# Turning the x tiles of a projection: TensorE transpositions, or VectorE's 32x32 blocks put together by transfers

## The chip, the cores and the metric

One core of a Trainium2 chip runs the whole program in one launch. The metric is the device time of a run in microseconds (us). The kernel before takes 3609.12 us in the median of three runs.

## What is computed

A transformer layer on x of shape [8, 1024, 512], float32. First attention with a low-rank latent (MLA): the layer-normed x is projected to a query latent and a key/value latent of 128 columns each and to a rotary key of 16. Sixteen heads are built from the latents, with causal softmax. Then a feed-forward part whose weights and activations are quantized to FP4 in blocks of 16 and dequantized again. Cut to what matters here:

```python
x = x + attn(layernorm(x), W_DQ, W_UQ, W_QR, W_DKV, W_UK, W_UV, W_KR, W_O)
x = x + ffn(layernorm(x), w_gate, w_up, w_down)

# in attn
c_q  = x @ W_DQ          # [B, S, 512] @ [512, 128]
c_kv = x @ W_DKV         # [B, S, 512] @ [512, 128]
Kr   = rope(x @ W_KR)    # [B, S, 512] @ [512, 16]
...
return attn @ W_O
# in ffn
h = silu(fp4_linear(x, w_gate)) * fp4_linear(x, w_up)
return fp4_linear(h, w_down)
```

The three products with x contract over its 512 columns, and TensorE contracts over partitions. So each normed tile of 128 rows x 512 columns must be turned: its columns have to come to lie along the partitions. The change is about this turning.

## The kernel before, in words

**Units.** The 8 x 1024 rows are cut into 16 units of 512 rows (`U`), two to a sequence: even units are the first half, odd ones the second. A unit is four tiles of 128 rows. While the attention of unit u runs (`attention`), the projections of unit u+1 are made (`project_pieces`), and so is a share of the feed-forward work of earlier units (`ffn_pieces`). An even unit has 4 quads of heads x 3 score steps, an odd one 4 x 7, and odd units take 13 parts of the feed-forward work where even ones take 5. In units 0 to 3 the raw feed-forward weights are quantized and turned in place of feed-forward work (`weight_pieces`: three loads and 34 pieces, which go through `turn`, line 186).

**The order.** The order on TensorE, VectorE and ScalarE is written out by hand. A piece is a pair of a cost and a function. `merged` interleaves a unit's own pieces with its share of other work, so that both lists advance by the same share of their cost. `attention` runs a score step and then pieces for as long as the cost of the pieces run, with half of the next one, stays below the share of the unit that its score steps have reached. A piece's cost so decides where it lands, and a cost that has no TensorE work behind it takes the place of some that has. A small model of time, `Clock`, decides where VectorE's deferred work (quantizing, adding up softmax sums) is laid in between. The order on SyncE's queue (SP), which issues nearly all DMAs, and on GpSimd is not written out: the framework chooses it, and places a DMA where its inputs and its buffer are ready.

**The projection of a unit** (`project_pieces`), for each of two pairs of tiles: `fetch` loads two x tiles (line 160, buffer tag xl, two buffers). `norms(0)` takes the statistics on VectorE (lines 320 to 322) and the power on GpSimd (323); `norms(1)` scales in place (326). `rows_turned` turns a tile with four TensorE transpositions into a PSUM bank and one ScalarE copy into xnT (`turn`, lines 186 and 188). `rotation` multiplies xnT by the rotary key weights (tile pr) and by the key/value latent weights (pp, wdkv); `rotated` does the query latent (pp, wdq) and the fold of the rotary key (pf). All TensorE products other than transpositions go through `mm` and have line 114.

**wo.** In the third score step of a unit's first quad, `fetch_wo` (lines 707 to 709) claims one of three softmax buffers (tag pT), which has to be given back by the product that reads it (num) and by the addition that sums it (line 599), and loads the 1 MB output weights into it. At the end of the same step `out_proj` multiplies by them (tile po), after `fillers` of that step:

```python
score_step(u, hq, j, qc, qr, acc, aT)
flush(1)
if urgent and j == 2:
    fetch_wo()
...
while fillers and (gone + fillers[0][0] / 2) * whole < total * spent:
...
while urgent and j == 2:
    urgent.popleft()()
```

`out_proj` loads x again (tag xo, 160), adds it on VectorE (728), and stores the sum to a DRAM tile mid (730), from which the feed-forward part reads it (y, line 747; xr, 823). `down` ends with the store of the result (852).

Of the kernel before, what the change touches and what calls it, by code (L numbers as in the profile page):

```python
# [11 lines left out]
F32 = mybir.dt.float32  # L12
# [6 lines left out]
P = 128  # L19
B, S, D = 8, 1024, 512  # L20
# [5 lines left out]
U = 512  # L26
NT = U // P
NDC = D // P
# [14 lines left out]
def tile_mla_then_fp4_ffn(  # L43
# [17 lines left out]
    nc = tc.nc  # L61
    const = ctx.enter_context(tc.tile_pool(name="const", bufs=1))
    p1 = ctx.enter_context(tc.tile_pool(name="p1", bufs=1))
    p2 = ctx.enter_context(tc.tile_pool(name="p2", bufs=2))
# [15 lines left out]
    class Clock:  # L80
# [3 lines left out]
        shape = None  # L84
# [23 lines left out]
    clk = Clock()  # L108

    def mm(dst, par=1, **kw):  # L110
        shape = kw.get("tile_position", ()) and "rows" or dst.shape[0]
        clk.pe += 0.00168 * dst.shape[-1] / par + (0.1 if shape != clk.shape else 0.0)
        clk.shape = shape
        nc.tensor.matmul(dst, **kw)  # L114

# [41 lines left out]
    def load_x(u, t, pool, tag):  # L157
        b, rows = rows_of(u, t)
        xt = pool.tile([P, D], F32, tag=tag, name=f"{tag}_{u}_{t}")
        nc.sync.dma_start(out=xt, in_=x[b, rows, :])  # L160
        return xt


    xls = {(0, t): load_x(0, t, p2, ("xl", "y")[t // 2]) for t in range(NT)}
    by_chunk = lambda w: w.rearrange("(c p) n -> p c n", p=P)
    by_head = lambda w: w.rearrange("p (h n) -> p h n", n=64)
    of_four = lambda w: w.unsqueeze(0).to_broadcast([4, *w.shape])
# [11 lines left out]
    def bank(name):  # L179
        return ps_t.tile([P, 512], F32, tag="t", name=name)  # L180

    def turn(src, dst, n):

        pt = bank("pt").rearrange("p (n k) -> p n k", k=P)
        for i in range(n):
            nc.tensor.transpose(pt[:, i, :], src[:, i * P : (i + 1) * P], ident)
            clk.pe += 0.11
        on_act(0.56, lambda: nc.scalar.copy(dst, pt[:, 0:n, :]))
# [123 lines left out]
    def normed(xt, key):  # L312
        got = {}

        def stats():
            pool, tag = (small, "nx") if key[0] == "x" else (p1, "ny")
            own = pool.tile([P, 10], F32, tag=tag, name=tag)
            st, ve = own[:, 0:6], own[:, 8:9]
            got["mv"], got["rstd"] = mv, rstd = own[:, 6:8], own[:, 9:10]
            nc.vector.bn_stats(st, xt)  # L320
            nc.vector.bn_aggr(mv, st)
            nc.vector.tensor_scalar(ve, mv[:, 1:2], EPS, None, ALU.add)
            nc.gpsimd.tensor_tensor(rstd, ve, neg_half, ALU.pow)

        def scaled():
            nc.vector.tensor_scalar(
                xt, xt, got["mv"][:, 0:1], got["rstd"], ALU.subtract, ALU.mult
            )

        return [(0.9, stats, key), (0.5, scaled, key)]  # L330
# [11 lines left out]
    def project_pieces(u):  # L342
        hf = u % 2
        state = {}

        def fetch(*ts):
            for t in ts:
                if (u, t) not in xls:
                    xls[u, t] = load_x(u, t, p2, "xl")

        def norms(k, *ts):

            for t in ts:
                if k == 0:
                    state["norm", t] = normed(xls[u, t], ("x", u, t))
                cost, run, _ = state["norm", t][k]
                clk.dve += cost
                run()
                state["ready", t] = clk.dve

        def rows_turned(t):
            g, k = divmod(t, 2)
            if k == 0:
                state["xnT"] = p1.tile([P, NDC, 256], F32, tag="xnT", name=f"xnT_{u}_{g}")
            normed_at = state["ready", t]
            clk.pe = max(clk.pe, normed_at)
            turn(xls.pop((u, t)), state["xnT"][:, :, k * P : (k + 1) * P], NDC)

        def latent(g, w, dst):
            cols = slice(g * 256, (g + 1) * 256)  # L370
            pp = bank("pp")
            for i in range(NDC):
                mm(
                    pp[:, :256],
                    lhsT=w[:, i, :],
                    rhs=state["xnT"][:, i, :],
                    start=(i == 0),
                    stop=(i == NDC - 1),
                )
            copy_out(dst[:, cols], pp[:, :256])  # L380

        def rotation(g):
            if g == 0:
                proj[u] = tuple(
                    pool.tile([P, U], F32, tag=tag, name=f"{tag}_{u}")
                    for pool, tag in ((p2, "cq"), (p2, "ckv"), (p3, "kr"))
                )
            pr = bank("pr")
            for i in range(NDC):
                mm(  # L390
                    pr[32 * i : 32 * i + 32, :256],
                    par=4,
                    lhsT=wkr[:, i, :],
                    rhs=state["xnT"][:, i, :],
                    start=True,
                    stop=True,
                )

            krp = proj[u][2][:, g * 256 : (g + 1) * 256]
            tab = rope_sb[:, hf * U + g * 256 : hf * U + (g + 1) * 256]  # L400
            on_dve(
                0.4, clk.pe + 0.3, lambda: nc.vector.tensor_tensor(krp, pr[:, :256], tab, ALU.mult)
            )
            state["krp"] = krp
            latent(g, wdkv, proj[u][1])

        def rotated(g):
            latent(g, wdq, proj[u][0])
            pf = bank("pf")
            for i in range(4):  # L410
                mm(
                    pf[32 * i : 32 * i + 32, :256],
                    par=4,
                    lhsT=fold_sb,
                    rhs=state["krp"],
                    start=True,
                    stop=True,
                )
            copy_out(proj[u][2][:, g * 256 : (g + 1) * 256], pf[:, :256])

        def both(*fs):
            for f in fs:
                f()

        if u == 0:
            for t in (0, 2):
                for k in range(2):
                    norms(k, t, t + 1)
            first, second = [], []
        else:  # L430
            first = [
                (1.0, lambda: fetch(0, 1)),
                (1.5, lambda: norms(0, 0, 1)),
                (3.0, lambda: norms(1, 0, 1)),
            ]
            second = [lambda k=k: norms(k, 2, 3) for k in range(2)]
        return [
            *first,
            (0.5, lambda: rows_turned(0)),
            (0.5, lambda: both(lambda: rows_turned(1), *[lambda: fetch(2, 3)] * (u > 0))),  # L440
            (2.3, lambda: both(lambda: rotation(0), *second[:1])),
            (2.2, lambda: both(lambda: rotated(0), *second[1:])),
            (2.0, lambda: None),
            (0.5, lambda: rows_turned(2)),
            (0.5, lambda: rows_turned(3)),
            (2.3, lambda: rotation(1)),
            (2.2, lambda: rotated(1)),
        ]
# [296 lines left out]
    def fetch(n):  # L745
        ys[n] = p2.tile([P, D], F32, tag="y", name=f"y_{n}")
        nc.sync.dma_start(out=ys[n], in_=mids[tiles[n]])
# [165 lines left out]
    n_weights = len(weight_work)  # L913
# [4 lines left out]
    for u in range(n_units):  # L918
        if u > 0:
            urgent.extend(lambda t=t, aTs=aTs: out_proj(u - 1, t, aTs) for t in range(NT))  # L920
        own = []
        if u + 1 < n_units:
            own.extend(project_pieces(u + 1))
            content, rotary = quad_pieces(u + 1, 0)
            own.extend([(1.7, content), (0.9, rotary)])
        take = []
        if u < FIRST:
            upto = n_weights * (5, 16, 20, 37)[u] // 37
            while weight_work and n_weights - len(weight_work) < upto:
                take.append(weight_work.popleft())  # L930

            for _ in range(6 if u == FIRST - 1 else 0):
                c, n, run = ffn.popleft()
                take.append((c, run, n))
        else:

            left = sum((13, 5)[v % 2 == 0] for v in range(u, n_units))
            within = sum(c for c, n, _ in ffn if n < len(tiles) - NT)
            budget = within * (13, 5)[u % 2 == 0] / left
            while ffn and budget > 0 and ffn[0][1] < NT * u:  # L940
                c, n, run = ffn.popleft()
                budget -= c
                take.append((c, run, n))
        fillers.extend(merged(own, take))
        aTs = attention(u)
        while fillers:
            fillers.popleft()[1]()
# [88 lines left out]
```

## Time and profile before

| | |
|---|---|
| median of three runs | 3609.12 us (3609.05 to 3610.31) |
| the profiled execution's own time | 3609.08 us |
| its span in the trace | 3607.3 us |
| mean granted TensorE clock | 0.995 of full speed |
| ScalarE, GpSimd busy | 35%, 19% |
| DMA engines busy, over the span | 11% (queue of SP) |
| packets of all DMAs; those under 512 B | 77190; 13852 |
| DMA of an x tile (xl, 256 KB), issue to landing | 2.7 us median |
| DMA of wo (1 MB), issue to landing | 5.1 us median |
| TensorE's waits for wo | 17.1 us, four times, 8.0 the longest |

The span runs from the first to the last instruction of one profiled execution; the time of a run has 1.8 us more around it. A group of the profile is written as line, engine, operation, output<-inputs, shape and count, then the group's busy time in us and the mean of one in ns, then the idle time of the engine just ahead of it with what ended most of it. PE is TensorE, PEld its weight loads (which overlap), DVE VectorE, ACT ScalarE, POOL GpSimd. SPq is the queue of SyncE. In a timeline a row is: start in us, length in us, engine, line, operation and tiles, count, and the wait ahead of it in brackets. In a table by stretch, a row is the stretch, its length, then the busy time of TensorE, its weight loads, VectorE, ScalarE and GpSimd with instruction counts, the granted clock, the DMA share and GB/s.

### The profile page before, as it was taken

To read this page: it belongs to the slowest core of one execution; us is meant where nothing else is said; L and a number is where in the kernel's file an instruction comes from. 1 tells how busy PE (TensorE), PEld (TensorE's weight loads), DVE (VectorE), ACT (ScalarE), POOL (GpSimd) and SP (SyncE) were. 2 spreads that over 40 slices of the span, in tenths; PEclk is the share of its full clock that TensorE was granted. 3 is DMA by queue.
4 is the path that set the end of the run, shared out by engine and by line. 5 is a ranking of instruction groups with operands and counts; after the bars stand their busy time and mean duration, and the time that the engine had idled before them with its cause. 6 is when DMAs were issued, how large, how long until landed. Compare 5 with 4: busy or idle time off the path is not lost.

```text
span 3607.3 us, 50032 instructions
## 1 busy us (share of the span) xinstructions
PE 3532.1 (98%) x19908; PEld 2038.8 (57%) x19908; DVE 2995.6 (83%) x5504; ACT 1265.2 (35%) x1778; POOL 670.1 (19%) x838
## 2 busy tenths in 40 slices
PE   8999899999999999999999999999999999999999
PEld 4334346656556566556666565655556555655576
DVE  6877858879988888888889888898878887879897
ACT  4443343333333333333333332333333332333311
POOL 3332231111111111211112111111111111112100
PEclk9999999999999999999999999999999999999999
DMA  3112101110010100011000101000110001010100
GB/s 95 62 39 72 34 13 53 45 33 24 18 58 19 53 24 24 30 47 47 24 24 19 59 21 53 21 24 33 45 47 24 24 12 59 18 47 15 50 30 15
DMA packets 77190, 131.50 MB, mean 36 GB/s; under 512 B 13852, under 2 KB 15388, under 8 KB 76956
## 3 DMA queue, kind: packets, MB, share of 16 engines
q1 hardware_dynamic: 75108, 127.43, 11.0%
q8 instruction: 157, 2.57, 0.3%
q10 hardware_dynamic: 1848, 0.87, 0.1%
q14 instruction: 77, 0.63, 0.1%
HBM read 94.72 MB, written 33.55 MB: 36 GB/s over the span
## 4 chain that ended last, share of the span: by engine, by line
PE 75%; DVE 8%; ACT 2%; issue 1%; POOL 0%; DMA 0%; ACTq 0%; POOLq 0%; DVEq 0%; SPq 0%
PE pg L114 32%; PE pd L114 13%; PE sc_ps L114 11%; PE num L114 5%; PE po L114 5%; PE pp L114 2%; PE den L114 1%; PE pk L114 1%; PE pqr L114 1%; PE pv L114 1%; PE pq L114 1%; DVE h L258 1%; ACT pT L555 1%; DVE pT L599 1%; DVE h L214 1%
## 5 line engine op out<-in xcount | busy, mean ns | idle before, releaser
L555 ACT ACTIVATE pT<-sc_ps 128x1024 f32<-128x1024 f32 (+1 forms) x640 | 566.3, 937 | 1119.2 <-PE sc_ps L114 987.0
L114 PE MATMUL pg<-yT,wu_T 128*128 128x256 f32 x2816 | 641.4, 381 | 3.5 <-ACT kT L127 1.4
L114 PE MATMUL pg<-yT,wg_T 128*128 128x256 f32 x2816 | 638.1, 382 | 1.6 <-ACT yT L765 1.0
L114 PE MATMUL pd<-wd_T,h 128*128 128x512 f32 x1408 | 618.9, 595 | 3.5 <-DVE h L214 3.5
L114 PEld LDWEIGHTS pg<-yT,wg_T 128*128 128x128 f32 x2816 | 528.1, 190 | 124.7 <-issue 39.5
L114 PEld LDWEIGHTS pg<-yT,wu_T 128*128 128x128 f32 x2816 | 526.3, 190 | 121.3 <-issue 39.9
L573 POOL TENSOR_SCALAR pT<-pT 128x1024 f32<-128x1024 f32 (+1 forms) x320 | 340.0, 1062 | 992.5 <-ACT pT L555 673.0
L577 POOL TENSOR_SCALAR_AFFINE_SELECT pT<-pT 128x256 f32<-128x256 f32 (+1 forms) x384 | 247.0, 643 | 1231.9 <-DVE pT L570 1021.6
L599 DVE TENSOR_TENSOR pT<-pT 128x1024 f32<-128x1024 f32 (+3 forms) x528 | 469.0, 912 | 6.2 <-POOL pT L577 2.8
L114 PEld LDWEIGHTS pd<-wd_T,h 128*128 128x128 f32 x1408 | 264.4, 190 | 343.0 <-issue 321.2
L570 DVE TENSOR_SCALAR pT<-pT 128x1024 f32<-128x1024 f32 (+1 forms) x320 | 207.8, 649 | 221.4 <-ACT pT L555 220.5
L114 PE MATMUL sc_ps<-qc,kT 32*128 32x512 f32 (+3 forms) x3072 | 341.0, 528 | 6.2 <-ACT pT L555 6.1
L127 ACT COPY h<-pg 128x512 f32<-128x512 f32 x192 | 105.8, 551 | 680.5 <-PE pg L114 680.5
L114 PE MATMUL num<-pT,v 128*32 128x512 f32 (+3 forms) x3072 | 321.4, 497 | 3.1 <-POOL pT L577 2.6
L114 PE MATMUL sc_ps<-qr,kr 32*128 32x512 f32 (+3 forms) x3072 | 307.2, 484 | 0.6 <-DVE qr L491 0.5
L258 DVE TENSOR_TENSOR h<-h,m 128x512 f32<-128x512 f32 (+1 forms) x384 | 263.0, 685 | 11.1
L214 DVE STREAM_TRANSPOSE h<-h 128x512 f32<-128x512 f32 (+1 forms) x384 | 250.6, 658 | 4.8
L114 PE MATMUL po<-wo,aT 128*128 128x512 f32 x512 | 229.4, 607 | 20.4 <-DMA wo<-in_w_o_dram 17.1
L114 PEld LDWEIGHTS sc_ps<-qc,kT 32*128 32x128 f32 x3072 | 114.9, 184 | 179.1 <-issue 118.6
L813 DVE TENSOR_TENSOR h<-pg,h 128x512 f32<-128x512 f32 x192 | 122.2, 638 | 110.1 <-PE pg L114 105.7
L114 PEld LDWEIGHTS sc_ps<-qr,kr 32*128 32x128 f32 x3072 | 145.4, 186 | 106.9 <-issue 82.2
L114 PEld LDWEIGHTS num<-pT,v 128*32 128x32 f32 x3072 | 66.4, 108 | 210.4 <-issue 147.8
(92 smaller groups left out, 3558.1 us busy)
## 6 DMA issues: line engine op xcount, KB each, us to landing
xo<-in_x_dram SPq DMA_DIRECT2D x64, 256.0 KB, 2.6
wo<-in_w_o_dram SPq DMA_DIRECT2D x16, 1024.0 KB, 5.1
mid<-xo SPq DMA_DIRECT2D x64, 256.0 KB, 2.1
y<-mid SPq DMA_DIRECT2D x64, 256.0 KB, 2.6
xr<-mid SPq DMA_DIRECT2D x64, 256.0 KB, 2.6
out_dram<-xr SPq DMA_DIRECT2D x64, 256.0 KB, 2.0
xl<-in_x_dram SPq DMA_DIRECT2D x62, 256.0 KB, 2.7
wraw<-in_w_gate_dram SPq DMA_DIRECT2D x11, 256.0 KB, 3.0
```

The costliest lines, as they stand in the source:

```text
L114: nc.tensor.matmul(dst, **kw)
L127: on_act(0.1 + 0.0009 * src.free_size(), lambda: nc.scalar.copy(dst, src))
L214: 0.06 + 0.0013 * part.shape[1], lambda: nc.vector.transpose(part, part), key
L258: nc.vector.tensor_tensor(part, part, got["m"], op)
L555: lambda: nc.scalar.activation(part, sc[:, 2 * k : 2 * k + 2, :cols], AF.Exp, scale=SM_SCALE),
L570: lambda: nc.vector.tensor_scalar(part, part, E_HI, E_LO, ALU.min, ALU.max),
L573: nc.gpsimd.tensor_scalar(part, part, E_HI, E_LO, ALU.min, ALU.max)
L577: nc.gpsimd.affine_select(out=diag, in_=diag, pattern=[[0, 2], [0, len(segs)], [1, P]], compare_op=ALU.is_ge, fill=0.0, base=0, channel_mu ...
L599: lambda a=whole, b=part: nc.vector.tensor_tensor(a, a, b, ALU.add),
L813: lambda: nc.vector.tensor_tensor(h, pg, h, ALU.mult),
```

## The change

In thirteen of the sixteen units (all but 0, 1 and 3) TensorE no longer turns x. A pair of x tiles is loaded by one DMA into one buffer (xp, one buffer where there were two of xl). After the scaling, VectorE transposes every 32x32 block of a tile in place. Then `settle` issues sixteen DMAs on SP, SBUF to SBUF. Each takes one group of 32 partitions and one of the four block columns, for both tiles and all four chunks of 128 columns, and puts it where the block belongs in xnT: 32 partitions x 8 runs of 32 floats. The layout of xnT changes from chunk by 256 rows to tile, chunk, 128 rows, so the products read two runs of 128 columns where they read one of 256. In units 0, 1 and 3 TensorE goes on turning, out of the new buffer. The own list of a settled unit has other costs: 5.0 for each `settle`, 1.5 for `norms(1)`. Of the 37 weight pieces 23 are done by the end of unit 2, before 20.

```diff
+    def pair_of_x(u, g):
+        return p1.tile([P, 2, D], F32, tag="xp", name=f"xp_{u}_{g}")
...
-        def fetch(*ts):
-            for t in ts:
-                if (u, t) not in xls:
-                    xls[u, t] = load_x(u, t, p2, "xl")
+        def fetch(g):
+            b = u // 2
+            r0 = hf * U + g * 2 * P
+            state["xp"] = xp = pair_of_x(u, g)
+            nc.sync.dma_start(
+                out=xp, in_=x[b, r0 : r0 + 2 * P, :].rearrange("(t p) d -> p t d", p=P)
+            )
+            xls.update({t: xp[:, t, :] for t in range(2)})
...
                 cost, run, _ = state["norm", t][k]
                 clk.dve += cost
                 run()
+                if k == 1 and not by_pe:
+                    clk.dve += 0.72
+                    nc.vector.transpose(xls[t], xls[t])
...
+        def settle(g):
+
+            state["xnT"] = xnT = p1.tile([P, 2 * NDC, P], F32, tag="xnT", name=f"xnT_{u}_{g}")
+            src = state["xp"].rearrange("p t (i q k) -> p (t i) q k", q=4, k=32)
+            for a in range(4):
+                for q in range(4):
+                    nc.sync.dma_start(
+                        out=xnT[32 * q : 32 * q + 32, :, 32 * a : 32 * a + 32],
+                        in_=src[32 * a : 32 * a + 32, :, q, :],
+                    )
+            state["there"] = max(clk.pe, clk.dve) + 13.0
+
+        def chunk(i):
+            return state["xnT"].rearrange("p (t c) k -> p c t k", t=2)[:, i]
...
-                    rhs=state["xnT"][:, i, :],
+                    rhs=chunk(i),
...
+            there = state.get("there", 0.0)
+            clk.pe = max(clk.pe, there)
...
+        by_pe = u in (0, 1, 3)
...
         return [
-            *first,
-            (0.5, lambda: rows_turned(0)),
-            (0.5, lambda: both(lambda: rows_turned(1), *[lambda: fetch(2, 3)] * (u > 0))),
-            (2.3, lambda: both(lambda: rotation(0), *second[:1])),
-            (2.2, lambda: both(lambda: rotated(0), *second[1:])),
-            (2.0, lambda: None),
-            (0.5, lambda: rows_turned(2)),
-            (0.5, lambda: rows_turned(3)),
+            (1.0, lambda: fetch(0)),
+            (1.5, lambda: norms(0, 0, 1)),
+            (1.5, lambda: norms(1, 0, 1)),
+            (5.0, lambda: settle(0)),
+            (1.0, lambda: fetch(1)),
+            (2.3, lambda: both(lambda: rotation(0), lambda: norms(0, 0, 1))),
+            (2.2, lambda: both(lambda: rotated(0), lambda: norms(1, 0, 1))),
+            (5.0, lambda: settle(1)),
             (2.3, lambda: rotation(1)),
             (2.2, lambda: rotated(1)),
         ]
...
-            upto = n_weights * (5, 16, 20, 37)[u] // 37
+            upto = n_weights * (5, 16, 23, 37)[u] // 37
```

More of the change, by code (lines that the diff above doesn't have):

```diff
@@ L111, in mm @@
         shape = kw.get("tile_position", ()) and "rows" or dst.shape[0]
-        clk.pe += 0.00168 * dst.shape[-1] / par + (0.1 if shape != clk.shape else 0.0)
+        clk.pe += 0.00168 * dst.free_size() / par + (0.1 if shape != clk.shape else 0.0)
         clk.shape = shape
@@ L161, in load_x @@
         return xt
-    xls = {(0, t): load_x(0, t, p2, ("xl", "y")[t // 2]) for t in range(NT)}
+    def pair_of_x(u, g):
+        return p1.tile([P, 2, D], F32, tag="xp", name=f"xp_{u}_{g}")
+    pair = pair_of_x(0, 0)
+    xls = {t: pair[:, t, :] for t in range(2)}
+    for t in range(2):
+        nc.sync.dma_start(out=xls[t], in_=x[0, t * P : (t + 1) * P, :])
+    xls.update({t: load_x(0, t, p2, "y") for t in range(2, NT)})
     by_chunk = lambda w: w.rearrange("(c p) n -> p c n", p=P)
@@ L354, in norms @@
                 if k == 0:
-                    state["norm", t] = normed(xls[u, t], ("x", u, t))
+                    state["norm", t] = normed(xls[t], ("x", u, t))
                 cost, run, _ = state["norm", t][k]
@@ L363, in rows_turned @@
             if k == 0:
-                state["xnT"] = p1.tile([P, NDC, 256], F32, tag="xnT", name=f"xnT_{u}_{g}")
+                state["xnT"] = p1.tile([P, 2 * NDC, P], F32, tag="xnT", name=f"xnT_{u}_{g}")
             normed_at = state["ready", t]
             clk.pe = max(clk.pe, normed_at)
-            turn(xls.pop((u, t)), state["xnT"][:, :, k * P : (k + 1) * P], NDC)
+            turn(xls.pop(t), state["xnT"][:, k * NDC : (k + 1) * NDC, :], NDC)
+        def settle(g):
[10 more added lines that the diff above has]
+            return state["xnT"].rearrange("p (t c) k -> p c t k", t=2)[:, i]
         def latent(g, w, dst):
@@ L373, in latent @@
                 mm(
-                    pp[:, :256],
+                    pp[:, :256].rearrange("p (t k) -> p t k", t=2),
                     lhsT=w[:, i, :],
-                    rhs=state["xnT"][:, i, :],
+                    rhs=chunk(i),
                     start=(i == 0),
@@ L390, in rotation @@
                 mm(
-                    pr[32 * i : 32 * i + 32, :256],
+                    pr[32 * i : 32 * i + 32, :256].rearrange("p (t k) -> p t k", t=2),
                     par=4,
                     lhsT=wkr[:, i, :],
-                    rhs=state["xnT"][:, i, :],
+                    rhs=chunk(i),
                     start=True,
@@ L428, in project_pieces @@
                     norms(k, t, t + 1)
[L429 to L432, printed above, removed]
+            return [
+                (0.0, lambda: rows_turned(0)),
+                (0.0, lambda: rows_turned(1)),
+                (0.0, lambda: rotation(0)),
+                (0.0, lambda: rotated(0)),
+                (0.0, lambda: rows_turned(2)),
+                (0.0, lambda: rows_turned(3)),
+                (0.0, lambda: rotation(1)),
+                (0.0, lambda: rotated(1)),
+            ]
+        if by_pe:
+            return [
+                (1.0, lambda: fetch(0)),
                 (1.5, lambda: norms(0, 0, 1)),
                 (3.0, lambda: norms(1, 0, 1)),
+                (0.5, lambda: rows_turned(0)),
+                (0.5, lambda: both(lambda: rows_turned(1), lambda: fetch(1))),
+                (2.3, lambda: both(lambda: rotation(0), lambda: norms(0, 0, 1))),
+                (2.2, lambda: both(lambda: rotated(0), lambda: norms(1, 0, 1))),
+                (2.0, lambda: None),
+                (0.5, lambda: rows_turned(0)),
+                (0.5, lambda: rows_turned(1)),
+                (2.3, lambda: rotation(1)),
+                (2.2, lambda: rotated(1)),
             ]
-            second = [lambda k=k: norms(k, 2, 3) for k in range(2)]
         return [
-            *first,
-            (0.5, lambda: rows_turned(0)),
-            (0.5, lambda: both(lambda: rows_turned(1), *[lambda: fetch(2, 3)] * (u > 0))),
-            (2.3, lambda: both(lambda: rotation(0), *second[:1])),
-            (2.2, lambda: both(lambda: rotated(0), *second[1:])),
-            (2.0, lambda: None),
-            (0.5, lambda: rows_turned(2)),
-            (0.5, lambda: rows_turned(3)),
+            (1.0, lambda: fetch(0)),
+            (1.5, lambda: norms(0, 0, 1)),
+            (1.5, lambda: norms(1, 0, 1)),
+            (5.0, lambda: settle(0)),
+            (1.0, lambda: fetch(1)),
+            (2.3, lambda: both(lambda: rotation(0), lambda: norms(0, 0, 1))),
+            (2.2, lambda: both(lambda: rotated(0), lambda: norms(1, 0, 1))),
+            (5.0, lambda: settle(1)),
             (2.3, lambda: rotation(1)),
```

## The prediction, made before the result

> **What bounds the kernel now.** I read the page's engine row and chain of work first, then the groups by line, the busy time by stretch and the timeline around one unit.
>
> ```profile
> PE 3532.1 (98%) x19908; PEld 2038.8 (57%) x19908; DVE 2995.6 (83%) x5504; ACT 1265.2 (35%) x1778; POOL 670.1 (19%) x838
> ...
> PE 75%; DVE 8%; ACT 2%; issue 1%; POOL 0%; DMA 0%; ACTq 0%; POOLq 0%; DVEq 0%; SPq 0%
> ```
>
> TensorE is idle for 75 us of 3607 and carries the chain; VectorE carries 8% of it. An average can hide a stage, so here are an odd unit (5) and an even one (6), cut at their value projections:
>
> ```profile
> 677.70:1011.00 333.30, 331.95 (x1758) 197.67 (x1758) 290.54 (x522) 121.10 (x165) 51.07 (x63) 1.00 0.10 31
> 1011.00:1176.00 165.00, 163.99 (x914) 99.13 (x913) 135.45 (x264) 56.70 (x85) 30.17 (x44) 1.00 0.12 41
> ```
>
> In both TensorE idles about 1 us and VectorE (fourth number) is busy 87% and 82%. So a microsecond taken from TensorE is a microsecond of the end; one added to VectorE mostly is not; every wait put in front of TensorE counts in full.
>
> **What is removed.**
>
> ```profile
> L186 PE MATMUL pt<-ident,xl 128*128 128x128 f32 x248 | 37.1, 282 | 9.1 <-DVE xl L326 6.4 <-DVE rc L657 2.1 <-ACT kT L127 0.6
> L114 PE MATMUL pr<-xnT,wkr 128*32 128x256 f32 x256 | 20.6, 394 | 5.9 <-ACT xnT L188 4.5 <-DVE xr L849 1.4
> ```
>
> One transposition has a latency of 282 ns, but they overlap: 37.1/248 = 0.150 us each. Thirteen units x 4 tiles x 4 = 208 of them: -31.1 us. The waits for their copy go too: 4.5 us here and 0.4 under pg and den, less 1.5 in unit 0, which stays: -3.4. The 6.4 us wait for xl is the start of unit 0 and stays. ScalarE loses 52 copies of 0.594 us, 31 us; at 35% busy that is worth nothing by itself.
>
> **What is added on VectorE.** The only block transposition of this shape in the groups kept apart by form takes 702 ns:
>
> ```profile
> L214 DVE STREAM_TRANSPOSE h<-h 128x512 f32<-128x512 f32 x320 | 222.7, 702 | 3.9
> ```
>
> 52 x 0.702 = 36.5 us, or 2.8 us in a unit. The cover is TensorE's streaming: odd units go from 87% to 88%. With the chain's 8% as the exposed share, +3 us (bounds 0 and 36).
>
> **What is added as transfers.** A pair becomes sixteen DMAs of 32 KB on SP, each 256 runs of 128 bytes: 4096 runs. The near row is the start, where three weight loads are 2048 runs of 128 bytes each (SP's timeline, then issue to landing):
>
> ```profile
> 3.74 0.66 SPq L173 DMA_DIRECT2D wuk<-in_w_uk_dram  x1
> 6.18 4.09 SPq L174 DMA_DIRECT2D wqc<-in_w_q_dram  x1
> 10.32 3.16 SPq L175 DMA_DIRECT2D wqr<-in_w_q_dram  x1
> ...
> wo<-in_w_o_dram SPq DMA_DIRECT2D x16, 1024.0 KB, 5.1
> ...
> wqr<-in_w_q_dram SPq DMA_DIRECT2D x1, 256.0 KB, 6.3
> ```
>
> 6144 runs went from 3.74 to 10.32 + 6.3 = 16.6: 12.9 us, 2.1 ns a run beside other loads. A pair: 8.6 us of data (0.54 per DMA), about 11 us with a first landing. A rule speaks against this: the Trainium skill, "VectorE: DVE Perf Modes", section "The three transpose paths", calls a plain DMA that transposes by strides 19 times slower than the crossbar's 1309 ns for a 128x128 block. The pair has eight blocks, so by the rule 8 x 19 x 1.3, an estimate of 199 us a pair, 5200 us in all, which no unit covers. But the rule is about a long stride of the innermost element; here VectorE has turned the inside of each 32x32 block, and the DMAs move runs of 128 bytes on both sides. The row is that shape (from memory outside the core, though), so I take 11 us.
>
> Is 11 us covered? The order follows from piece costs: own pieces of a unit sum to 26.6 (before 21.1), and TensorE's first use comes 6 of 26.6 after the transfer step, 22%; the second 19%. In an even unit (about 160 us) that is 30 to 35 us, in odd ones 60 or more. So the new TensorE wait, with everything queued behind it, costs 0 (above 0 only from three times my price). Sixteen completions to wait for may add 51 ns semaphore steps to TensorE's queue: between 0 and 26 x 15 x 0.051 = 20 us. The trace already has 308 under L114 without an idle row of their own, so 0.
>
> On SP the next pair's load now waits until all sixteen have read the tile; behind it stand mid stores and y, xr and xo loads. Those have tens of us; wo does not.
>
> **The step that pays: wo.** wo is fetched into a freed pT buffer and used at once. Unit 6:
>
> ```profile
> 1031.72 0.55 DVE L326 TENSOR_SCALAR xl<-xl,nx 128x512 f32<-128x512 f32 x1 [0.44 <-POOL nx L323]
> 1032.18 0.95 DVE L599 TENSOR_TENSOR pT<-pT 128x768 f32<-128x768 f32 x1
> 1033.68 0.92 DVE L599 TENSOR_TENSOR pT<-pT 128x768 f32<-128x768 f32 x1
> 1033.98 0.85 PE L114 MATMUL num<-pT,v 128*32 128x384 f32 x8
> 1034.76 3.72 PE L114 MATMUL pg<-yT,wg_T 128*128 128x256 f32 x16
> 1034.93 0.38 SPq L709 DMA_DIRECT2D wo<-in_w_o_dram  x1
> 1038.32 3.62 PE L114 MATMUL pg<-yT,wu_T 128*128 128x256 f32 x16
> 1041.78 0.59 PE L114 MATMUL po<-wo,aT 128*128 128x512 f32 x1
> ```
>
> wo leaves when num and the second addition have let the buffer go, lands 5.1 us later at 1040.0, and is wanted at 1041.8: 1.8 us to spare, because two groups of pg lie between. Replaying the interleaving by the code's costs: the third attention step, the one ahead of po, may bring the pieces run to 25% of the unit's 109.0, so 27.3. The first two have used 17.1 (load 1.0, down 9.6, norms 3.0, gate 3.5); now the transfer step's 5.0 comes next, then a gate of 3.5 makes 25.6, and the following up (taken only if half of its 3.5 fits) just misses. Before, that step held gate and up, the two groups above. Units 4, 6, 8, 10 and 12 all lose one group so. In unit 6 po is then wanted at about 1038.4: a 1.6 us stall. Two transpositions before the additions release the buffer 1.2 us later. And the sixteen DMAs are ready at about 1033.4, ahead of wo on the same queue. At SP's 0.4 us apiece about four get in, and their remaining data delays wo by 0.8. Together 3.6 us in each of four units, 14.4; unit 4 (wo at 539.9, po at 545.1 after a 1.0 wait, two groups cut to one) loses 3.5 + 1.4 + 0.8 = 5.7. Sum +20 us. Bounds: 10 if wo goes first and the additions are no later, 44 if all sixteen stand ahead. Odd units keep two groups or more in that step; unit 14's feed-forward work is held back there before and after alike.
>
> **Weights.** Three pieces move from unit 3 to unit 2. Unit 3 waits 13.2 us for raw weights (L186 on wraw), unit 2 waits 8.0 for wo. The gap that the transfer step leaves crowds the remaining pieces in unit 3 about as before, so 0, between -13 and +5.
>
> **Sum.** The profiled run is 3609.1 us (span 3607.3 and 1.8 around), the median of the runs 3609.12: no difference. 3609.1 - 31.1 - 3.4 + 3 + 20 = 3597.6, called 3597.5; 8 to either side from the semaphore steps and the weights.
>
> **Rivals.**
> 1. wo keeps its place ahead of the transfers and only the lost cover is paid: 4 x 1.6 + 3.5 = 10. 3609.1 - 34.5 + 3 + 10 = 3587.6, lower if the weights gain. For it: wo stands earlier in program order. Against: its buffer comes free after the pair is ready.
> 2. Slower: SP issues all sixteen before wo. They leave from 1033.4 at 0.5 us each, so wo at 1041.6, behind data until 1044; it lands near 1047.5, 9 us after it is wanted. 4 x 9 + 8 in unit 4 = 44, and in five odd units the burst falls on out_proj's own xo loads, 2 us each: +54. 3609.1 - 34.5 + 3 + 54 = 3631.6. It decides from about ten transfers ahead of wo. For it: SP has issued loads as soon as they could go (xl for unit 1 at 15.5 us). Against: wo is written earlier, and would have to come ready late by the whole burst.
> 3. The transposed tile lands late. From 35 us after the blocks are turned, each further us costs 12 us over six even units with two pairs each: 3610 when it is 1 us late, 3650 at 4. The 2.1 ns row speaks against it.
> 4. VectorE becomes the bound and half of its 36 us shows: 3609.1 - 34.5 + 18 + 20 = 3612.6. Its idle 17% speaks against it.
>
> **Chances.** Forecast 0.45 (own range 3589 to 3606), rival 1 0.25, rival 2 0.18, rival 3 0.07, rival 4 0.05. A measurement can tell about 0.2%, 7 us. Faster: all of rival 1 and four fifths of the forecast, 0.61. Same: the rest of the forecast and some of rivals 2 to 4, 0.16. Slower: 0.23. Range 3577 to 3627: it leaves out the far end of rival 1 and most of rival 2.
>
> **What would show it.** L186 on x falls from 256 (248 xl, 8 y) to 48 and its 31 us go; a block transposition on xp appears x52 near 0.70 us; sixteen DMAs a pair land within about 11 us; pr waits for no DMA; and po's wait for wo grows from 17 us (four times) to about 37, in units 4 to 12. I am wrong if po's wait stays at 17, if pr waits for xnT, or if idle time shows elsewhere on TensorE.

## The result, and the profile after

The changed kernel takes 3726.70 us in the median of four runs (3718.33 to 3731.81), the kernel before 3609.09 us beside it: a ratio of 1.0324 with an interval of 1.0304 to 1.0343. It is 3.2% slower, where the forecast was 0.3% faster and the range ended at 3627. The profiled execution took 3731.81 us, its span is 3730.1 us.

Here are the engine row and the shares of the chain, from the page after:

```profile
PE 3557.4 (95%) x19700; PEld 2040.2 (55%) x19700; DVE 3030.0 (81%) x5556; ACT 1238.5 (33%) x1726; POOL 680.0 (18%) x838
...
PE 72%; DVE 10%; ACT 1%; DMA 1%; issue 1%; POOL 1%; SPq 0%; DVEq 0%; POOLq 0%; ACTq 0%
```

TensorE has 208 instructions fewer and is busy 25 us longer. Its idle time grew from 75 to 3730.1 - 3557.4 = 173 us. So there are two things to explain: 98 us of waiting, and matmuls that take longer. TensorE's waits name the first (engine, line and tile that waits, what released it: us in total, times, longest). First before, then after:

```profile
PE po L114 <- DMA wo<-in_w_o_dram: 17.1, 4, 8.0
PE pd L114 <- DVE h L214: 3.5, 7, 0.9
PE pt L760 <- DVE y L240: 3.0, 1, 3.0
```

```profile
PE po L114 <- DMA wo<-in_w_o_dram: 53.4, 10, 8.0
PE pd L114 <- DVE h L221: 38.3, 17, 6.4
PE pt L810 <- DVE y L247: 34.0, 10, 5.0
```

The three grew by 36, 35 and 31 us, 102 together; all other waits fell by 5. So they are the whole of the idle growth. The first is the wait that the prediction priced. The other two are waits of the feed-forward part for VectorE, for tiles that the change does not touch. They show where the odd units went as well. The busy time by stretch for units 5 and 6, cut at the copies of their value projections, first before, then after (the prediction's cut at 1011.0 lies 10 us ahead of that point, so its two lengths differ from these):

```profile
678.57:1021.51 342.94, 341.59 (x1781) 202.04 (x1780) 299.60 (x541) 121.45 (x166) 52.87 (x65) 1.00 0.10 30
1021.51:1177.32 155.81, 154.80 (x893) 95.16 (x892) 126.91 (x244) 55.77 (x84) 28.37 (x41) 1.00 0.13 43
```

```profile
686.81:1052.84 366.03, 348.13 (x1757) 204.09 (x1756) 293.69 (x528) 119.10 (x161) 57.11 (x65) 0.96 0.11 31
1052.84:1216.74 163.90, 155.10 (x877) 93.96 (x876) 135.14 (x259) 53.59 (x80) 29.42 (x41) 0.98 0.18 47
```

The odd unit, where nothing was expected to wait, lost 23 us; TensorE waits 17.1 us in it for h and y, and before not at all. VectorE's busy time in it (fourth number after the stretch) fell from 299.6 to 293.7 us: it is not overloaded, its work comes in another order. The granted clock, 1.00 in both units before, is 0.96 and 0.98.

What the change itself does came out nearly as predicted (groups of the page kept apart by form, and the DMA issues):

```profile
L193 PE MATMUL pt<-ident,xp 128*128 128x128 f32 x40 | 6.8, 312 | 7.1 <-DVE xp L333 6.5 <-ACT kT L127 0.6
L114 PE MATMUL pr<-xnT,wkr 128*32 128x256 f32 x256 | 20.8, 394 | 1.5 <-ACT xnT L195 1.5
L372 DVE STREAM_TRANSPOSE xp<-xp 128x512 f32<-128x512 f32 x52 | 37.0, 712 | 1.8
...
wo<-in_w_o_dram SPq DMA_DIRECT2D x16, 1024.0 KB, 5.7
xnT<-xp SPq DMA_DIRECT2D x416, 32.0 KB, 2.0
```

The group that turns x fell by 30.3 us (31.1 predicted; what this frees on TensorE is less, as shown further down), pr waits for no transfer, and the blocks take 0.712 us each.

### The profile page after: what moved, and what is told of

Same layout as the page of the kernel before. It is cut to its first block, busy times and chain, and to the rows that moved or that the text cites. A ratio compares the mean times of both kernels' runs of the same rounds, so it can differ in the third digit from the quotient of the medians.

```text
span 3730.1 us, 50178 instructions
## 1 busy us (share of the span) xinstructions
PE 3557.4 (95%) x19700; PEld 2040.2 (55%) x19700; DVE 3030.0 (81%) x5556; ACT 1238.5 (33%) x1726; POOL 680.0 (18%) x838
## 4 chain that ended last, share of the span: by engine, by line
PE 72%; DVE 10%; ACT 1%; DMA 1%; issue 1%; POOL 1%; SPq 0%; DVEq 0%; POOLq 0%; ACTq 0%
PE pg L114 30%; PE pd L114 12%; PE sc_ps L114 11%; PE po L114 5%; PE num L114 5%; PE pp L114 2%; DMA wo<-in_w_o_dram 1%; PE pk L114 1%; PE pqr L114 1%; PE pv L114 1%; DVE h L265 1%; PE den L114 1%; DVE h L221 1%; PE pq L114 1%; DVE pT L649 1%
## 5 line engine op out<-in xcount | busy, mean ns | idle before, releaser
L114 PE MATMUL pd<-wd_T,h 128*128 128x512 f32 x1408 | 637.9, 608 | 38.3 <-DVE h L221 38.3
L114 PE MATMUL pg<-yT,wu_T 128*128 128x256 f32 x2816 | 652.5, 387 | 0.1
L114 PEld LDWEIGHTS pg<-yT,wg_T 128*128 128x128 f32 x2816 | 532.7, 191 | 125.5 <-issue 37.1
L114 PEld LDWEIGHTS pg<-yT,wu_T 128*128 128x128 f32 x2816 | 535.2, 193 | 116.2 <-issue 31.2
L623 POOL TENSOR_SCALAR pT<-pT 128x1024 f32<-128x1024 f32 (+1 forms) x320 | 351.9, 1100 | 967.8 <-ACT pT L605 743.7
L114 PE MATMUL po<-wo,aT 128*128 128x512 f32 x512 | 242.8, 636 | 54.1 <-DMA wo<-in_w_o_dram 53.4
L265 DVE TENSOR_TENSOR h<-h,m 128x512 f32<-128x512 f32 (+1 forms) x384 | 259.3, 675 | 10.9
L114 PEld LDWEIGHTS po<-wo,aT 128*128 128x128 f32 x512 | 103.7, 205 | 186.3 <-issue 163.7
```

The source lines that it names most:

```text
L265: nc.vector.tensor_tensor(part, part, got["m"], op)
L623: nc.gpsimd.tensor_scalar(part, part, E_HI, E_LO, ALU.min, ALU.max)
```

## The experiments

The theory after the result: the loss is the hand-written order. The interleaving by costs and the modelled VectorE time put VectorE's deferred quantizing elsewhere, so that h and y come late. In the expectations it is theory P as far as the places of pieces go, and theory M with the modelled time. The rivals: VectorE's 37 us of added work is what makes them late (V); the sixteen transfers of a pair are (Q); the moved weight pieces are. Kernels measured together ran on one chip beside the kernel before, so each ratio is against that; its median was between 3609.5 and 3612.6 us.

**The places of pieces.** e1 is the changed kernel with costs of own pieces by which the feed-forward work falls about where it was before. e2 is its opposite: the new costs, with TensorE turning everything.

```diff
e1: -(1.5, norms(1)), (5.0, settle(0)), (1.0, fetch(1)) ... (5.0, settle(1))
    +(3.0, norms(1)), (1.0, both(settle(0), fetch(1))) ... (3.0, settle(1))
e2: -clk.dve += 0.72; nc.vector.transpose(xls[t], xls[t])
    -settle(g)
    +both(rows_turned, rows_turned)   # at 5.0, as settle
```

> The changed kernel with the costs of the own pieces set so that feed-forward pieces land where they did before (norms 3.0, settle and the next load 1.0, second settle 3.0; sum 21.1). Transfers and block transpositions stay. Theory P (places: the new costs take feed-forward groups from under wo and bunch VectorE's work): po's wait for wo falls from 53 to below 30 us, pd's wait for h and pt's for y from 72 to below 15, time about 3580 to 3600. Rival V (VectorE's 37 us of block transpositions make it late): pd and pt keep about 70 us, time about 3680. Rival Q (the sixteen transfers hold wo back on SP): po keeps 40 us or more, time about 3620 or more.

> The new costs and places, but every unit's tiles are turned by TensorE (no block transpositions, no transfers). Theory P: pd and pt still wait some 70 us and po about 35, granted clock near 0.98, time 3690 to 3740. Rival V: pd and pt wait below 15 us, time about 3620. Rival Q: po waits about 17 to 25 us only and the time is near 3610 to 3630.

e1: 3686.84 us, 1.0212 (1.0197 to 1.0228); waits for wo 35.3, h 22.9, y 16.0. e2: 3645.13 us, 1.0096 (1.0079 to 1.0113); wo 24.3, h 25.3, y 11.9. Both miss theory P's numbers. With the places near the old ones e1 still waits 39 us for h and y, where less than 15 was expected, and is 77 us above before. e2 has no block transposition and no settling transfer, and waits 37 us for h and y, where some 70 was expected. So the new costs are worth some 35 us without the new work (e2 keeps the moved weights and the single x buffer too), but the places do not explain the whole: something else is in the order.

**VectorE's work and the number of transfers.** e3 leaves the block transpositions out, so its projections read blocks that are not turned. e4 moves a pair by one DMA of 512 KB, so the blocks are not put in their places. All else stays, the 0.72 us in the model too.

```diff
e3: -nc.vector.transpose(xls[t], xls[t])
e4: -for a in range(4): for q in range(4): nc.sync.dma_start(...)
    +nc.sync.dma_start(out=xnT, in_=state["xp"].rearrange("p t (i k) -> p (t i) k", k=P))
```

> The changed kernel without VectorE's block transpositions (left out: the turning inside the 32x32 blocks, so the projections get wrong numbers); costs, places and transfers stay. Theory P: pd and pt keep 50 us or more, time above 3690. Rival V: pd and pt fall below 15 us and the time to about 3640. Rival Q: little change, about 3720, po's wait stays at 53.

> The changed kernel with one DMA of 512 KB a pair in place of sixteen (left out: the putting together of the blocks, so the projections get wrong numbers); costs, places and block transpositions stay. Theory P: po's wait falls from 53 to about 30 (the lost cover stays), pd and pt keep about 70, time about 3690 to 3705. Rival V: as P for pd and pt. Rival Q: po's wait falls to about 17 and the time to below 3650.

e3: 3719.12 us, 1.0302 (1.0287 to 1.0317), waits for h 39.1 and y 34.0. e4: 3716.42 us, 1.0293 (1.0278 to 1.0308), h 38.7, y 34.0, wo 43.4. The waits for h and y do not move when 37 us of VectorE work or 15 of 16 transfers go. Both rivals are worth some 10 us each of the 117 at most; e3's interval overlaps that of the changed kernel.

**The terms of the model.** f1 is the changed kernel without the jump of 13 us in the modelled TensorE time, f2 without the 0.72 us for each block, f3 is e1 without the jump. f4 is the idea alone: the costs, the modelled time and the weights of before, so that TensorE, VectorE and ScalarE keep the order of before; only the turning is replaced.

```diff
f1, f3: -state["there"] = max(clk.pe, clk.dve) + 13.0
        -clk.pe = max(clk.pe, there)
f2:     -clk.dve += 0.72
f4:     f1's and f2's, 20 weight pieces, and
        +(3.0, norms(1)), (0.5, as_turned(0)), (0.5, both(as_turned(1), settle(0), fetch(1))),
        +... (2.0, None), (0.5, as_turned(0)), (0.5, both(as_turned(1), settle(1))),
        # as_turned only moves the modelled time, as four transpositions and a copy did
```

> The changed kernel without that jump of the modelled time. Theory M: little here, since pieces worth more than 13 us lie between a settle and the products in full units: 3710 to 3727; the difference is in the model's two other terms. If the jump is what disorders VectorE: below 3680.

> The changed kernel with the block transpositions not counted in the modelled VectorE time (0.72 us each). Theory M with this term as cause: pd and pt fall from 72 to about 40 us, as under the costs alone, time about 3670. If the term does nothing: 3720 to 3727. Rival V: no change, since the work is the same.

> As e1 (feed-forward in its old places) without the jump of the modelled TensorE time to 13 us after a settle. Theory M: the waits behind kr (22 us under e1) go, and with them much of pd and pt; time 3600 to 3630, against 3687. Rival V and rival Q: about 3680, as e1.

> The idea alone: the written-out order on TensorE, VectorE and ScalarE is that of before, instruction by instruction, and so are its weights (20) and modelled clock; only the transpositions of thirteen units and their copies are out and the block transpositions and sixteen transfers in. Theory M (the new order that the modelled clock works out for VectorE, and the places, cost the time; blocks and transfers cost little): pd and pt wait below 15 us, kr for nobody, po for wo about 30, time 3585 to 3600. Rival V (VectorE's extra work): pd and pt wait 40 us or more, time 3640 or more. Rival Q (transfers): po waits 45 us or more, time about 3620.

f1: 3720.52 us, 1.0308 (1.0293 to 1.0323). f2: 3660.41 us, 1.0143 (1.0128 to 1.0158), h 24.4, y 11.9. f3: 3667.58 us, 1.0157 (1.0142 to 1.0172). f4: 3611.78 us, 1.0004 (0.9995 to 1.0013), h 3.5, y 3.0, wo 33.8. The jump is small here (6 us, within the noise; 19 with e1's costs, which leaves f3 far above the 3600 to 3630 expected). The 0.72 us in the model are worth 66 us. f4's waits:

```profile
PE po L114 <- DMA wo<-in_w_o_dram: 33.8, 8, 8.4
PE pd L114 <- DVE h L221: 3.5, 7, 0.9
PE pt L814 <- DVE y L247: 3.0, 1, 3.0
```

With the order of before the waits for h and y are those of before, with all blocks and transfers in place. In time nothing is lost, and nothing is gained, where 3585 to 3600 was expected: the wait for wo doubled (+17), and TensorE is busy only 12 us less (3519.7 for 3532.1), as part of what the turning frees goes to a slower clock (shown further down).

**The count by itself.** In f2 and the changed kernel the new places are there too. g3 counts the 0.72 us in f4. h1 counts them in the kernel before, which has no block transposition at all. In both, TensorE's and ScalarE's orders stay.

```diff
g3 (on f4): +clk.dve += 0.72
h1 (on the kernel before, in norms): +if k == 1 and u not in (0, 1, 3):
                                     +    clk.dve += 0.72
```

> The idea alone in the old order (f4_old_order), and only the 0.72 us for each block transposition added to the modelled VectorE time. TensorE's and ScalarE's orders stay the same, instruction by instruction; VectorE's deferred work is laid elsewhere. If the counted time is what makes quantized h and y late, the waits pd on h and pt on y grow (from 3.5 and 3.0 us to 15 to 40 and 10 to 30) and the time grows by 20 to 60 us, to 3632 to 3672. If counting costs only together with the new places of the pieces, the time stays at 3608 to 3616.

> The kernel before, with its TensorE transpositions and no block transposition at all: only the modelled VectorE time is put forward by 0.72 us for each x tile of thirteen units. No instruction is added or taken away; TensorE's and ScalarE's orders are the same, VectorE's deferred work is laid later. If the order that the model writes is the cause, po's wait stays at 17 us, the waits for h and y grow to about 20 us each as in g3, and the time is 30 to 50 us above before: 3640 to 3660. If the loss in g3 comes from the block transpositions' own time on VectorE, this kernel stays within 7 us of before.

g3: 3655.70 us, 1.0129 (1.0113 to 1.0145). h1: 3658.38 us, 1.0132 (1.0115 to 1.0148). Both times are as the first of the two expectations has it (wo's wait in h1 grew to 23.0 us, though it was to stay at 17). h1 executes the same instructions as the kernel before. In its trace TensorE's and ScalarE's orders are those of before, and some 1300 of VectorE's 5504 instructions stand elsewhere. TensorE's waits in h1:

```profile
PE po L114 <- DMA wo<-in_w_o_dram: 23.0, 6, 8.3
PE pd L114 <- DVE h L214: 19.8, 21, 2.1
PE pt L762 <- DVE y L240: 19.8, 5, 4.7
```

How such a wait comes about is read from one y tile in unit 5; the others were not followed one by one. First the timeline of the kernel before, then that of h1: L326 norms the tile, L244 is the first pass that rewrites it to quantize it, the last row turns it.

```profile
859.78 0.55 DVE L326 TENSOR_SCALAR y<-y,ny 128x512 f32<-128x512 f32 x1 [0.75 <-POOL ny L323]
862.58 0.69 DVE L244 SCALAR_TENSOR_TENSOR y<-y,rs 128x512 f32<-128x512 f32 x1
...
877.00 0.60 PE L760 MATMUL pt<-ident,y 128*128 128x128 f32 x4
```

```profile
861.24 0.55 DVE L326 TENSOR_SCALAR y<-y,ny 128x512 f32<-128x512 f32 x1 [0.67 <-POOL ny L323]
...
873.46 0.69 DVE L244 SCALAR_TENSOR_TENSOR y<-y,rs 128x512 f32<-128x512 f32 x1
...
880.02 1.08 PE L762 MATMUL pt<-ident,y 128*128 128x128 f32 x4 [3.79 <-DVE y L240]
```

Before, the rewriting follows the norm by 2.2 us (862.58 - 860.33). In h1 it begins 11.7 us after it, and the transposition waits 3.79 us. The reason is read from the code, not from a run. `fill` lays deferred work only where the modelled VectorE has a gap ahead of the next urgent instruction, and what it has not laid is laid by `need`, right where the tile is used. An account that is later by 0.72 us a tile has fewer gaps, so more work is left to `need`.

h3 puts the count the other way in g2 (below): `clk.dve -= 0.72`.

> The kernel g2_wo_on_scalar with the modelled VectorE time set back by 0.72 us for each turned tile, so that deferred work is laid earlier; TensorE's and ScalarE's orders are the same. If the model holds deferred work back for longer than VectorE needs, the last waits for h and y (3.5 and 3.0 us) go and urgent work is not late: 3595 to 3603. If the old order is already the best balance, urgent work comes late and the time rises: 3608 to 3640.

h3: 3611.41 us, 0.9999 (0.9991 to 1.0008), where g2 has 0.9983. The waits for h and y stay at 3.5 and 3.0 us; num waits 10.7 us for GpSimd's pT instead of 4.7. This is nearer the second expectation: work laid earlier than before gains nothing. A loss of 0.15% is not shown, as the intervals of the two runs just touch.

**Where wo stands.** g1 and g2 are f4 with wo's load issued by GpSimd or ScalarE instead of SP. h2 is the kernel before with wo on ScalarE. i1 is f4 with wo on ScalarE only in units 4, 6, 8, 10 and 12, where transfers of xnT stood ahead of it.

```diff
-nc.sync.dma_start(out=outs["wo"], ...)
+nc.gpsimd.dma_start(out=outs["wo"], ...)   # g1
+nc.scalar.dma_start(out=outs["wo"], ...)   # g2, h2; i1: if u in (4, 6, 8, 10, 12)
```

> The kernel with the idea alone in the old order (f4_old_order), and wo's load issued by GpSimd instead of SyncE: TensorE's, VectorE's and ScalarE's orders are the same, instruction by instruction. If wo is late because it stands behind transfers of xnT on SyncE's queue, po's wait for wo falls from 33.8 us to about 17 to 20, the stalls and the slow clock behind them go with it, and the time falls from 3611.8 to about 3585 to 3595, under the kernel before. If wo is late because its data shares the DMA engines with the transfers, or because its buffer comes free late, the wait stays at 30 us or more and the time at 3608 to 3615.

> As g1, but ScalarE issues wo's load. By the theory of the queue the wait for wo falls as in g1, to 17 to 20 us; ScalarE has to wait for the buffer ahead of two copies of h, so 0 to 10 us may come back: 3585 to 3600. By the theory of shared DMA engines nothing falls: 3608 to 3620.

> The kernel before, with wo's load issued by ScalarE; all else the same. Before, nothing stands ahead of wo on SyncE's queue, so if g2 gains by letting wo pass the transfers, this kernel gains nothing: 3606 to 3614, po's wait near 17 us. If ScalarE's queue is better for wo by itself, it gains 5 us or more, below 3604, and the turning has no part in g2's gain.

> The idea alone in the old order (f4_old_order), with wo's load on ScalarE's queue only in the units where xnT's transfers stood ahead of it (4, 6, 8, 10, 12), and on SyncE's queue in the others. If g2's gain came from those units and its loss from the others (h2 lost 9 us by ScalarE's queue in the kernel before), po's wait falls from 33.8 us to 20 to 25 and the time to 3588 to 3598, below before. If the two can't be had apart, it stays at g2's 3602 to 3607.

g1: 3611.38 us, 1.0005 (0.9998 to 1.0012), wo 35.2: one miss. In units 6 to 12 its waits for wo fall below 0.8 us each, but the other units pay (10.2 us in unit 2, 8.1 in unit 14), as GpSimd's issue takes 0.81 us and wo 5.8 to land. g2: 3604.82 us, 0.9983 (0.9974 to 0.9992), wo 29.0, between its two expectations. h2: 3621.61 us, 1.0025 (1.0015 to 1.0034), wo 25.5, outside both: ScalarE's queue itself is a loss of 9 us. i1: 3589.97 us, 0.9945 (0.9932 to 0.9959), which is 22 us below the kernel before on its chip (3611.93) and the fastest of all. Its engine row and wait for wo:

```profile
PE 3508.8 (98%) x19700; PEld 2017.1 (56%) x19700; DVE 3024.8 (84%) x5556; ACT 1237.4 (34%) x1726; POOL 668.9 (19%) x838
```

```profile
PE po L114 <- DMA wo<-in_w_o_dram: 21.4, 7, 8.3
```

Against the span of before, TensorE is busy 23 us less and idle 3 us more (78.4 for 75.2): 20 us, the difference of the spans. Against f4 the wait for wo is 12.4 us shorter, and TensorE's busy time 10.9 us. So the idea pays as far as the order is kept and wo does not queue behind its transfers.

**The weights.** e6 is the changed kernel with 20 weight pieces by the end of unit 2 (`(5, 16, 20, 37)`).

> The changed kernel with 20 weight pieces by the end of unit 2, as before, instead of 23. If the weights are a side matter, as predicted, the time is that of the changed kernel within 10 us: 3717 to 3737. If crowding the third unit's weights is part of the loss, it falls by 13 us or more, below 3714.

e6: 3728.26 us, 1.0330 (1.0314 to 1.0346). The weights are no cause of the loss.

## Why the prediction was wrong

**The step that failed** is in the sum's "+3" for VectorE and in what stood behind it: the prediction took every change of the costs as a change of wo's cover only, and left VectorE's order as it was. It replayed the interleaving for TensorE, found one group of pg fewer under wo, and stopped. It gave `clk.dve += 0.72` no step at all, though the modelled time decides where deferred work is laid. What the runs showed in its place: waits of TensorE for h and y that grew from 6.5 to 72.3 us, made by the order and not by VectorE's work. By the runs, in ratios to before: the count alone 1.3% (h1), 46 us; the new places of the pieces alone 1.0% (e2), 35 us; both on top of the idea 1.0324 - 1.0004 = 3.2% (changed kernel against f4), 115 us. They are not additive: after the count the places (with the jump and the moved weights) cost 1.0324 - 1.0129 = 2.0%, without it 1.0143 - 1.0004 = 1.4%. The prediction named the sign that came: "if idle time shows elsewhere on TensorE".

**Rival 4** has the right engine and the wrong reason. It let VectorE become the bound by its 36 us; e3 takes this work away and is 7.6 us faster of 117, with intervals that overlap. VectorE's idle share even grew, from 17% to 19%.

**The turning's size.** The prediction divided the group's busy time by its count, 0.150 us for a transposition, and took 31.1 us. But these rows overlap those of their neighbours. Here are four transpositions in the timeline before, with the row ahead of them and the one behind:

```profile
468.07 1.13 PE L114 MATMUL pqr<-cq,wqr 128*128 128x512 f32 x2
469.04 0.60 PE L186 MATMUL pt<-ident,xl 128*128 128x128 f32 x4
469.57 0.39 PE L114 MATMUL sc_ps<-qc,kT 32*128 32x128 f32 x4
```

Of their 0.60 us only 469.20 to 469.57, 0.37 us, is theirs alone. Over the whole trace TensorE has nothing but these transpositions under way in 26.4 of the group's 37.1 us, so 208 of them free about 22 us, not 31. i1, whose clock is that of before (0.994 for 0.995), agrees: TensorE is busy 23 us less there.

**wo.** The mechanism is right, its size was off. Predicted: +20 us, four transfers ahead of wo at 0.4 us each, one group of pg left. Measured: +36 us, of which 34 in units 4 to 12. Unit 6 in the timeline of the changed kernel (SP's rows are issues, x8 is eight DMAs):

```profile
1064.13 6.14 SPq L389 DMA_DIRECT2D xnT<-xp  x8
1064.83 0.85 PE L114 MATMUL num<-pT,v 128*32 128x384 f32 x8
1065.49 0.92 DVE L649 TENSOR_TENSOR pT<-pT 128x768 f32<-128x768 f32 x1
1065.61 3.72 PE L114 MATMUL pg<-yT,wg_T 128*128 128x256 f32 x16
1070.44 0.48 SPq L759 DMA_DIRECT2D wo<-in_w_o_dram  x1
1070.96 6.16 SPq L389 DMA_DIRECT2D xnT<-xp  x8
1076.65 15.82 PE L114 MATMUL po<-wo,aT 128*128 128x512 f32 x32 [7.32 <-DMA wo<-in_w_o_dram]
```

One group covers wo, as replayed. But eight transfers are ahead of it (twelve in unit 4), and they follow each other by 0.77 us (6.14/8), so wo leaves 6.3 us after the first of them, and 4.0 us after num and the second addition have let its buffer go (1066.4). The stall of 7.3 us was predicted as 3.6. In the old order, with two groups as cover, the same queueing still costs 16.7 us (f4), and i1 removes 12.4 of these. Rival 2 has the right place and comes near the size (44 us for 36), but the wait's growth is less than a third of the loss.

**A term that the sum lacked: the clock behind a stall.** The same stall by stretch (the granted clock stands ahead of the DMA share and GB/s, which end the row):

```profile
1069.34:1073.55 4.21, 0.00 (x0) 0.00 (x0) 2.60 (x4) 0.59 (x1) 0.44 (x1) 1.00 0.48 111
1073.55:1076.65 3.10, 0.00 (x0) 0.03 (x1) 0.00 (x0) 0.00 (x0) 0.00 (x0) 0.50 1.21 288
1076.65:1080.38 3.73, 3.73 (x5) 1.66 (x6) 0.00 (x0) 0.00 (x0) 0.00 (x0) 0.50 0.12 13
1080.38:1084.00 3.62, 3.62 (x10) 1.62 (x9) 1.66 (x6) 0.00 (x0) 0.00 (x0) 1.00 0.06 24
```

TensorE falls idle at 1069.34; 4.2 us later the clock drops to 0.50, and it stays there for 6.83 us, of which the last 3.73 are work. The 32 products of po took 15.82 us, before 13.90 without the stall, so this stall costs about 2 us more than its length. The Trainium skill, "TensorE: Matmul & The Clock Gate", section "What's actually happening", has both ends of this: half the clock after at least one idle window of about 3.4 us, the full one again after about 3.4 us of work. The trace agrees on the half and on the window: the changed kernel has 27 stretches at 0.50 behind its stalls, each of 3.41 us or two or three times that, where before has 6. It does not agree that a whole window must be idle: a stall of 2.3 us (from 3518.4) had such a stretch behind it, while others of up to 2.9 us had none. In these stretches TensorE works 122 us, before 25, and half of the difference, 48 us, is lost. That is what its busy time shows: 25 us more, although the turning freed about 22, so 47. The idle time and the busy time, 98 + 25 = 123 us, are the difference of the two spans (3730.1 - 3607.3).

**What was right.** The group of the turning (-30.3 for -31.1), its copies (pr's wait from 4.5 to 1.5 us), the blocks (0.712 for 0.702 us), the weights (e6), and the cover of the transfers: a pair lands in about 13 us rather than 11, and pr waits for none of them. The 199 us a pair of the rule that the prediction set aside did not come. (The 1309 ns in it are for bf16 by the page's table, which the prediction did not say.) The gain is real too, 22 us in i1. That i1's 3589.97 is close to rival 1's 3587.6 is luck: i1 loses no cover and frees less turning than rival 1 counted.

**What stays open.** Why the new places alone (e2) make h and y late was not traced to single pieces, and which of `fill` and `need` laid the late passes was not recorded. The sizes of the two order effects hold for this model and these costs.

## What to carry to other kernels

Where a program's order comes out of a cost model, every number of the model in a diff is a change of the schedule: ask what is laid by it and who waits for that, even if no instruction differs (h1). To price an idea, put it in with the order held fixed first (f4), and only then let the planner see it. Before a burst of DMAs goes on a queue, find the load that has to leave on that queue while the burst lasts, and count a stall of several microseconds on TensorE with the slow clock behind it (2.3 us of lost work for each stretch at 0.50 here, 61 us for 27). To price an instruction that leaves a busy engine, take the time in which nothing else is under way, not its row's length.

## What the hardware showed that was not expected

An SBUF-to-SBUF DMA of 256 runs of 128 bytes took 0.61 us to issue on SP, where a load of wo took 0.38, so a pair's sixteen are bound by the issue: 10.4 us for an undisturbed pair, of about 13 to the last landing. One DMA for a whole pair (e4) still gained only 10 us in 26 pairs. wo from ScalarE's queue made the kernel before 9 us slower (h2), with 8.4 us more of waiting for wo, though there are no transfers to pass: in unit 1 ScalarE issues it just behind the start of an activation, at 103.6 us, where SP did at 101.5.
